# A fused attention kernel: work moved between VectorE and GpSimd at its two ends, and one transpose moved inside its loop

## The chip, the core and the metric

The kernel runs on one core of a Trainium2 chip. The core has five engines that run side by side, each with its own instruction queue: TensorE (PE in the profile) multiplies matrices from SBUF into PSUM; VectorE (DVE) does element-wise work, reductions and 32x32 block transposes; ScalarE (ACT) does exponentials, copies and scalings; GpSimd (POOL) does element-wise work on SBUF; SyncE (SP) mostly issues DMA transfers. ScalarE and GpSimd can issue DMAs from their queues too. Engines wait for each other by semaphores.

The metric is the device time of one execution in microseconds. Times are medians over runs.

## The reference

Self-attention with 16 heads of 32 columns over 8 sequences of 512 rows, with a conditioning vector that is projected by the same W_q and W_k and added to every row of Q and K, and the input added to the result:

```python
Q = _split_heads(x @ Wq.T + bq)
K = _split_heads(x @ Wk.T + bk)
V = _split_heads(x @ Wv.T + bv)
tQ = _split_heads(tokens @ Wq.T + bq)
tK = _split_heads(tokens @ Wk.T + bk)
cQ = Q + tQ
cK = K + tK
scores = jnp.einsum('bhqd,bhkd->bhqk', cQ, cK) / jnp.sqrt(jnp.float32(HEAD_DIM))
attn = jax.nn.softmax(scores, axis=-1)
out = jnp.einsum('bhqk,bhkd->bhqd', attn, V)
...
x = x + out
```

`x` is (8, 512, 512), `tokens` is `cond_1024[:, None, :]` of (8, 1, 512), all float32.

## The kernel before

**Tiles and steps.** The work is cut into 32 tiles `t`: batch `t // 4`, and within it four heads, one from each 128-column block of the model dimension. A tile's K and Q lie transposed in SBUF (`qkT`), so that the four heads sit on the four groups of 32 partitions. Projections are made for pairs of tiles with a scheme of seven half-size products (`product`, L459) whose sums of x blocks (`xc`) and of weight blocks (`wc`) are made by GpSimd (`combine_w`, L353 to L356; `combine_x`, L385 to L389).

**Two ways to the softmax.** For every tile the scores are computed with queries on partitions (`row_scores`, L617), and VectorE takes their negated row maxima (`one_max` L584, `row_max_of` L626). Then the tiles go two ways:
- Odd tiles up to 27 (`BLOCKED`): ScalarE takes the exponentials from these scores (`denominators`, L664) into the `arena`, DMAs regroup them by 32 partitions into `blocks` (`exchange`, L648, on the queues of SyncE and GpSimd), and VectorE transposes the 32x32 blocks in eight units of 128x1024 (`turn_blocks`, L637). TensorE multiplies them by V (`times_v`, L745).
- Even tiles, and the last four: the maxima are split into three bf16 parts (`split_max`, L678 to L681: cast, subtract, cast, subtract, each needing the one before). They are turned by a DMA (`turn_max`, L694), or in the last tiles by TensorE (`transpose_max`, L704, and a copy at L710). The scores are then computed again with keys on partitions, the maxima being added by TensorE (L720, L723), and exponentiated (`exponentials`, L734).

**The loop** runs over steps t = 1 to 28, each with four quarters (items V, q, k, v): quarter 0 multiplies the previous tile's exponentials by V and sends its rows out; quarters 1 to 3 make a product of q, k or v for a later batch. In each quarter the row maxima of one quarter of the next tile are taken, and, where due, a transposition of `blocks`. How many units follow which quarter stands in a small table, `TURNED`, keyed by (step minus tile, quarter). `split_max` for the next tile stands in quarter 2 directly behind its maxima, ahead of that quarter's units.

**Order.** The instruction order on TensorE, ScalarE, VectorE and GpSimd is the program's order, written out by hand; a framework adds the semaphores. Each engine executes its queue strictly in order.

**The start.** The first rows of W_q and the first half of x of batch 0 are loaded by SyncE and ScalarE. GpSimd makes the identity matrix `ident`, then issues DMAs for the two biases (into `cond_sp`, L285) and for the first rows of W_k (`load_first`, L244). VectorE builds `which`, `modulo` and `identb` from memsets and `ident` (L315 to L323), then transposes W_q's rows, the first half of x (L889), W_k's rows (L334), the second half of x (L889), and the conditioning rows (L905), scales the biases (L909, L910), and finishes the conditioning terms `tok` (L860, L861). These are added when q and k are copied out of PSUM (q on VectorE, L415; k on ScalarE, L417). SyncE's queue loads the second half of x, the conditioning vectors (L301), and then the whole of W_q, W_k and W_v.

**The end.** Tiles 30 and 31 have no `blocks`. Their denominators are sums of the four exponential tiles (two halves `pr` each, 128x1024), made by `sum_of` (L1147 for the first two tiles, L1149 for each further one) into `acc` (tile 30) and `acc2` (tile 31), and then multiplied by ones on TensorE (`times_ones`, L755). In `acc`, one half of the first sum is made by GpSimd and the rest by VectorE. GpSimd's last two operations scale tile 30's result and add the residual (L1274, L1275). `send_parts` (L813, L814 on GpSimd) sends tile 29 out just before. Tile 31's result is turned back by TensorE (L1304, L836), divided and stored by VectorE and four DMAs (L1309 to L1321).

Of the kernel before, what the change touches and what calls it, by code (L numbers as in the profile page):

```python
# [9 lines left out]
F32 = mybir.dt.float32  # L10
BF16 = mybir.dt.bfloat16
AF = mybir.ActivationFunctionType
ALU = mybir.AluOpType
# [4 lines left out]
def kernel(  # L18
# [38 lines left out]
    nc = tc.nc  # L57
    P = 128
# [182 lines left out]
    def load_first(n, a, queues):  # L241

        for h in range(HG):
            queues[h].dma_start(  # L244
                first[n][h * BL : (h + 1) * BL].rearrange("p k c e -> p k (c e)"),
                a.rearrange("(k g j) d -> g j k d", g=G, j=BL)[0, :, :, h * P : (h + 1) * P],
            )

    def load_all(to, a, queues, fs=slice(0, NB)):

        for h in range(HG):
            queues[h].dma_start(
                to[h * BL : (h + 1) * BL, fs].rearrange("p f c e -> p f (c e)"),
                spread(a, h * P, NC)[:, fs],
            )
# [23 lines left out]
    load_first("q", Wq, two_queues)  # L279
    load_all(x0, x[0], two_queues, half_of_x[0])  # L280
    nc.scalar.activation(table, table, AF.Exp)
    ident = const.tile([P, P], F32, tag="ident", name="ident")
    make_identity(nc, ident)
    for i, bias in enumerate((bq, bk)):
        nc.gpsimd.dma_start(  # L285
            cond_sp[B + i :: BL, :P], bias.rearrange("(h c) -> h c", h=HG)
        )
    load_first("k", Wk, [nc.gpsimd] * HG)

    def rows_of(n, g):  # L290
        return first[n] if g == 0 and n in first else ws[n].rearrange("p (h g) c e -> p g h c e", g=G)[:, g]
# [7 lines left out]
    for h in range(HG):  # L299
        r = slice(h * P, (h + 1) * P)  # L300
        nc.sync.dma_start(cond_sp[h * BL : h * BL + B, :P], cond[:, r])  # L301
    load_all(ws["q"], Wq, [nc.sync] * HG)
    load_all(ws["k"], Wk, [nc.sync] * HG)
    load_all(ws["v"], Wv, [nc.sync] * HG)
# [6 lines left out]
    nc.vector.memset(m, 0.0)  # L311
    split = [m, m]

    which = const.tile([P, NS], F32, tag="which", name="which")
    nc.vector.memset(which, 0.0)  # L315
    modulo = const.tile([P, BL], F32, tag="modulo", name="modulo")
    for i in range(NS):
        r = slice(i * BL, (i + 1) * BL)
        nc.vector.memset(which[r, i : i + 1], 1.0)
        nc.vector.tensor_copy(modulo[r, :], ident[r, r])  # L320
    condT = early[:, 7, : NC * HD].rearrange("p (c e) -> p c e", e=HD)
    identb = const.tile([P, P], BF16, tag="identb", name="identb")
    nc.vector.tensor_copy(identb, ident)  # L323
    xc = const.tile([P, 4, 2, HS], F32, tag="xc", name="xc")
    vs = [const.tile([P, NS, D], F32, tag=f"v{i}", name=f"v{i}") for i in range(2)]

# [305 lines left out]
    def turn_blocks(t, units):  # L632

        for n in units:
            pr = slice(n % NP * 2, n % NP * 2 + 2)
            e = blocked[t][:, :, n // NP, pr, :].rearrange("p g h s -> p g (h s)")
            nc.vector.transpose(e, e)  # L637
# [207 lines left out]
    def condition(n, gs, pt):  # L845

        i = "qk".index(n)
        r = slice(gs[0], gs[-1] + 1)
        w = len(gs) * HD
        for cc in range(NC):  # L850
            for h in range(HG):
                nc.tensor.matmul(
                    pt[h * HD : (h + 1) * HD, :w],
                    condT[:, cc, :],
                    wT[n][:, cc, :].rearrange("p (g h e) -> p g h e", h=HG, e=HD)[:, r, h, :],
                    start=(cc == 0),
                    stop=(cc == NC - 1),
                )
        t = early[:, 1 + i, :w]
        nc.vector.transpose(t, pt[:, :w])  # L860
        nc.vector.tensor_tensor(  # L861
            tok[:, i, r],
            t.rearrange("p (g b) -> p g b", b=HD)[:, :, :B],
            bias2[:, i, r].unsqueeze(2).broadcast_to([P, len(gs), B]),
            ALU.add,
        )
        if gs[-1] == G - 1:
            nc.gpsimd.tensor_tensor(apart_tok[:, i], tok[:, i, 1::2], tok[:, i, 0::2], ALU.subtract)
# [40 lines left out]
    nc.vector.tensor_scalar(bias2[:, 0, :], condT[:, :, B], 2.0 * SCALE, None, ALU.mult)  # L909
    nc.vector.tensor_scalar(bias2[:, 1, :], condT[:, :, B + 1], 2.0, None, ALU.mult)  # L910
    project(0, "k", pk, two[1])
    condition("q", [0], bank(6))
    condition("k", [0], bank(5))
    project_qk_end(0, "q", pq, two[0])
# [140 lines left out]
            four_products(n, b, r // 2, dens, small, 0)  # L1055
            released(2, 3, 4, 5, 6, 7, 1, 0)

    TURNED = {(-1, 3): 1, (0, 0): 1, (0, 1): 2, (0, 2): 1, (0, 3): 3}
    turned = {1: 1}
    turn_blocks(1, range(1))  # L1060

    def turn_more(t, i):

        for u in (t - 1, t, t + 1):
            if u in BLOCKED and (t - u, i) in TURNED:
                n = turned.get(u, 0)
                turned[u] = n + TURNED[t - u, i]
                turn_blocks(u, range(n, turned[u]))

    ORDERS = {  # L1070
        (1, 0): [],
# [9 lines left out]
    for t in range(1, T - 3):  # L1081
        b, r = divmod(t, G)
        blocks = t in BLOCKED
        w = 0 if blocks else HG
        items = ["V", "q", "k", "v"]
        for i, item in enumerate(items):
            rows = (t + 1, i + 1) if i < 3 else (t + 2, 0)
            begin(w)
            if not blocks:
                exponentials(t, i)  # L1090
            late_first = item in ("v" if blocks else "qkv") and t % 2 == 1
            hold = row_max(*rows, late_first, w)

            def held(i=i, hold=hold):
                hold()
                if i == 2:
                    split_max(t + 1)
                    turn_max(t + 1)

            dens = lambda: denominators(*rows, w)  # L1100
            if item in "qkv":
                products(t, item, blocks, held, dens, nothing)
            else:
                held()
                dens()
                if blocks:
                    weighted(t - 1, banks(4), banks(5), nothing)
                    released(6, 7, 0, 1, 2, 3, 5, 4)
                else:
                    weighted(t - 1, banks(0), banks(1), nothing)  # L1110
                    released(2, 3, 1, 4, 5, 6, 7, 0)
            if i == 0 and r % 2 == 0:
                turn_x(t + NC + 2)
                turn_x(t + NC + 3)
            if i == 0 and r == 1:
                combine_x(b + 1, 1, nc.gpsimd)
            if i == 1 and r == 0:
                combine_x(b + 1, 0, nc.gpsimd)
            if i == 2:
                aparts[t] = masked(t)  # L1120
            turn_more(t, i)
# [33 lines left out]
    def row(i):  # L1155
        turn[0] = 8 + i
# [79 lines left out]
    part_of(t, banks(2), [0])  # L1236
    send_parts(t - 1, den)
    store()
    row(2)
    crossed(t, 2, 3)  # L1240
    split_max(t + 1, nc.vector)
    pa, rest = banks(2), [1, 2, 3]
    times_v(t, 1, pa, rest)

    exponentials(t, 3, (0, 1, 7, 4))
    transpose_max(t + 1, bank(5), nc.vector.tensor_copy)
    times_v(t, 2, pa, rest)
    sum_of(t, acc, 1, nc.vector, [0])
    sum_of(t, acc, 2, nc.vector)

    t = T - 1
    exponentials(t, 0, (2, 3, 0, 1))
    times_v(t - 1, 3, pa, rest)
    nc.vector.tensor_tensor(parts[t - 1], pa, parts[t - 1], ALU.add)
    sum_of(t - 1, acc, 3, nc.vector)
    exponentials(t, 1, (7, 4, 5, 2))
    pv = bank(3)
    times_v(t, 0, pv)
# [1 line left out]
    sum_of(t, acc2, 1, nc.vector)  # L1260
    exponentials(t, 2, (0, 1, 7, 6))
    times_v(t, 1, pv)
    pd = bank(5)
    times_ones(acc, pd, True, True)
    sum_of(t, acc2, 2, nc.vector)
    den = late_part(9).rearrange("p (f e) -> p f e", e=BL)
    nc.vector.transpose(den.rearrange("p f e -> p (f e)"), pd)

# [2 lines left out]
    y30 = late_part(13).rearrange("p (f e) -> p f e", e=BL)  # L1271
    nc.vector.transpose(y30.rearrange("p f e -> p (f e)"), parts[t - 1])
    x30 = xr.pop(t - 1)
    nc.gpsimd.tensor_tensor(y30, y30, rec.broadcast_to([P, NB, BL]), ALU.mult)  # L1274
    nc.gpsimd.tensor_tensor(y30, y30, x30, ALU.add)  # L1275

    def store_30(queue, hs):
        b, g = divmod(t - 1, G)
        for h in hs:
            queue.dma_start(spread(out[b], h * P + g * BL), y30[h * BL : (h + 1) * BL])  # L1280

    store_30(nc.sync, (0, 1))
    exponentials(t, 3, (4, 2, 0, 1))
    times_v(t, 2, pv)
    pd = bank(7)
    times_ones(acc2, pd, True, False)
# [4 lines left out]
    nc.vector.tensor_tensor(part_x, pd, xr[t], ALU.mult)  # L1291
    den = late_part(11)
    nc.scalar.copy(den, pd)
    store_30(nc.scalar, (2,))
    oT = late[0][:, 0, :]
    y = late[0][:, 1, :].rearrange("p (c s) -> p c s", c=NS)
    rec = op.tile([P, NS, HG, 1], F32, tag="rec", name="rec")
# [3 lines left out]
    for i in range(2):  # L1301
        nc.vector.tensor_tensor(oT[:, two[i]], pv[:, two[i]], part_x[:, two[i]], ALU.add)
# [6 lines left out]
    nc.vector.reciprocal(  # L1309
        rec, pi.rearrange("p (c h e) -> p c h e", c=NS, h=HG)[:, :, :, 0:1]  # L1310
    )
# [45 lines left out]
```

## Time and profile before

| | |
|---|---|
| median of 3 runs | 681.87 us (679.42 to 683.93) |
| the profiled execution | 680.71 us |
| its span, first to last instruction | 678.5 us |
| granted TensorE clock, mean | 0.995 |
| busy: TensorE, VectorE, ScalarE, GpSimd | 97%, 85%, 80%, 50% |
| instructions | 22874 |

The profile is one execution, recorded by the hardware. A row of its timeline gives the start and the length in us, the engine, the line of the kernel, the operation with its output and input tiles, the shape and the count (x2 where two of a kind follow each other), and in brackets how long the engine stood idle before and what ended that. An engine name with q is the part that issues DMAs. The chain of waits is followed back from the last instruction: at each step to what released it. A row of the table by stretches gives a window, its length and the busy time of TensorE, its weight loads, VectorE, ScalarE and GpSimd in it, then the granted clock, the share of the DMA engines and GB/s.

### The profile page before, as it was taken

The page shows a single profiled execution, that of the slowest core. Times are in us where ns is not written, and L with a number is a line of the kernel's source. Part 1 is how long each engine was busy: PE and PEld are TensorE (multiplying, and loading weights), DVE is VectorE, ACT ScalarE, POOL GpSimd, SP SyncE. Part 2 cuts the span into 40 slices and gives each one's busy share as a digit, 9 for nine tenths or more (in the row PEclk, how much of TensorE's full clock was granted, in tenths as well). Part 3 has the DMA queues.
Part 4 walks back from the last instruction along what each step waited for, and adds up shares of the span by engine and source line. Part 5 has one row for each costly group of instructions (what it writes and reads, how often), then busy time and mean ns, then how long its engine had stood idle before and what let it go on. Part 6 is the DMA issues. An engine that isn't in the chain of part 4 may idle for free.

```text
span 678.5 us, 22874 instructions
## 1 busy us (share of the span) xinstructions
PE 658.8 (97%) x9100; PEld 312.5 (46%) x9100; DVE 576.4 (85%) x821; ACT 541.9 (80%) x1397; POOL 340.0 (50%) x449
## 2 busy tenths in 40 slices
PE   7989999999999999999999999999999999999993
PEld 6444454544544444454545445444544445444421
DVE  4897988989898888979888897988889797887793
ACT  1568797988979798897979889797988979797771
POOL 5551563565446464465635654464644656352531
PEclk9999999999999999999999999999999999999998
DMA  9719427486483838658383865739386573812002
GB/s 200 133 24 211 127 60 208 95 207 146 123 195 86 221 82 206 147 129 208 74 224 74 209 143 133 196 73 232 73 214 139 132 181 68 222 42 56 16 17 32
DMA packets 140814, 90.85 MB, mean 134 GB/s; under 512 B 117436, under 2 KB 126308, under 8 KB 140708
## 3 DMA queue, kind: packets, MB, share of 16 engines
q1 hardware_dynamic: 132196, 73.78, 46.7%
q0 software_dynamic: 5568, 14.95, 8.6%
q8 instruction: 72, 1.18, 0.8%
q10 hardware_dynamic: 2944, 0.66, 0.4%
q14 instruction: 34, 0.28, 0.1%
HBM read 20.27 MB, written 8.39 MB: 42 GB/s over the span
## 4 chain that ended last, share of the span: by engine, by line
PE 80%; DMA 4%; DVE 3%; SPq 2%; ACT 1%; issue 1%; POOL 0%; DVEq 0%; ACTq 0%
PE psum L459 35%; PE psum L617 17%; PE psum L745 16%; PE psum L723 7%; PE psum L720 3%; DMA blocks<-arena 2%; SPq L648 2%; DMA wT_v<-split 1%; DVE nmax L626 1%; DVE nmax L584 1%; PE psum L1175 1%; PE psum L755 1%; DMA out_dram<-xr 0%; DVE blocks L637 0%; ACT arena L664 0%
## 5 line engine op out<-in xcount | busy, mean ns | idle before, releaser
L664 ACT ACTIVATE psum<-psum,nmax 128x512 f32<-128x512 f32 x256 | 169.1, 664 | 60.0 <-DVE nmax L584 47.5
L584 DVE TENSOR_REDUCE nmax<-psum 128x1 f32<-128x512 f32 x270 | 170.5, 676 | 47.9 <-PE psum L617 47.2
L734 ACT ACTIVATE arena<-psum 128x512 f32<-128x512 f32 x264 | 136.5, 602 | 32.9 <-PE psum L723 25.5
L617 PE MATMUL psum<-kT,qT 32*128 32x512 f32 x1024 | 156.1, 620 | 1.4 <-ACT psum L664 1.4
L664 ACT ACTIVATE arena<-psum,nmax 128x512 f32<-128x512 f32 x224 | 153.0, 704 | 1.2 <-DVE nmax L626 0.3
L626 DVE TENSOR_REDUCE nmax<-psum 128x2 f32<-128x1024 f32 x115 | 139.2, 1211 | 1.1 <-PE psum L617 1.1
L637 DVE STREAM_TRANSPOSE blocks<-blocks 128x1024 f32<-128x1024 f32 x112 | 133.0, 1216 | 0.2
L648 POOL DMA_DIRECT2D blocks<-arena x112 | 55.9, 504 | 76.3 <-ACT arena L664 66.7
L813 POOL TENSOR_TENSOR res<-res,recs 128x512 f32<-128x512 f32 x30 | 31.4, 1048 | 121.7 <-DVE res L812 121.7
L617 PEld LDWEIGHTS psum<-kT,qT 32*128 32x128 f32 x1024 | 58.9, 182 | 64.4 <-issue 28.4
L745 PE MATMUL psum<-arena,v 128*32 128x512 f32 x576 | 69.4, 597 | 0.0
L723 PE MATMUL psum<-qT,kT 32*128 32x512 f32 x528 | 68.1, 587 | 0.0
L745 PE MATMUL psum<-blocks,v 128*32 128x256 f32 x896 | 52.2, 381 | 0.0
L664 ACT ACTIVATION_READ_ACCUMULATOR psum<-psum,nmax 128x1 f32 x256 | 52.1, 204 | 0.0
L459 PE MATMUL psum<-wc_v,xc 128*32 128x256 f32 x768 | 50.6, 381 | 1.4 <-ACT v L497 1.4
L664 ACT ACTIVATION_READ_ACCUMULATOR arena<-psum,nmax 128x1 f32 x224 | 49.7, 222 | 0.0
L459 PE MATMUL psum<-xc,wc_q 128*32 128x256 f32 x720 | 47.4, 381 | 0.0
L459 PE MATMUL psum<-xc,wc_k 128*32 128x256 f32 x720 | 47.4, 381 | 0.0
L814 POOL TENSOR_TENSOR xr<-res,xr 128x512 f32<-128x512 f32 x30 | 38.4, 1281 | 2.4
L812 DVE STREAM_TRANSPOSE res<-psum 128x512 f32<-128x512 f32 x28 | 20.1, 717 | 22.8 <-PE psum L745 22.8
L207 POOL TENSOR_TENSOR xr<-xr,wT_q 128x512 f32<-128x512 f32 x30 | 38.3, 1277 | 0.2
L745 PEld LDWEIGHTS psum<-blocks,v 128*32 128x32 f32 x896 | 27.1, 110 | 24.4 <-ACT arena L734 10.6
(184 smaller groups left out, 933.7 us busy)
## 6 DMA issues: line engine op xcount, KB each, us to landing
blocks<-arena SPq DMA_DIRECT2D x336, 128.0 KB, 3.8
blocks<-arena POOLq DMA_DIRECT2D x112, 128.0 KB, 3.8
xr<-in_x_dram SPq DMA_DIRECT2D x60, 128.0 KB, 2.6
x<-in_x_dram SPq DMA_DIRECT2D x56, 128.0 KB, 3.6
out_dram<-xr SPq DMA_DIRECT2D x56, 128.0 KB, 2.3
w_q<-in_L_cond_Wq_dram SPq DMA_DIRECT2D x4, 256.0 KB, 4.2
w_k<-in_L_cond_Wk_dram SPq DMA_DIRECT2D x4, 256.0 KB
w_v<-in_L_cond_Wv_dram SPq DMA_DIRECT2D x4, 256.0 KB, 8.4
```

Source lines behind the costliest of these rows:

```text
L207: nc.gpsimd.tensor_tensor(xr[t], xr[t], bias, ALU.add)
L459: nc.tensor.matmul(pt[r], still[:, r], moving, start=(kc == kcs[0]), stop=(kc == kcs[-1]))
L584: nc.vector.tensor_reduce(nmax[t][:, qc, j : j + 1, 0], pt, AX.X, ALU.max, negate=True)
L617: nc.tensor.matmul(pt, qkT["q", t][r, qc * P : (qc + 1) * P], qkT["k", t][r, :], start=True, stop=True,)
L626: nc.vector.tensor_reduce(nmax[t][:, qc, pr * 2 : pr * 2 + 2, 0], pt, AX.X, ALU.max, negate=True)
L637: nc.vector.transpose(e, e)
L648: queue.dma_start(to.rearrange("p c h s -> p (c h s)"), of)
L664: nc.scalar.activation(to, of, AF.Exp, bias=nmax[t][:, qc, j, :], accum_out=sums[t][:, qc, j, :],)
L723: nc.tensor.matmul(bank[j], qkT["k", t][r, kc * P : (kc + 1) * P], qkT["q", t][r, :], start=False, stop=True,)
L734: nc.scalar.activation(e[:, i, :], bank[pr * 2 + i], AF.Exp)
L745: nc.tensor.matmul(pt[j * HD : (j + 1) * HD, at], vs[b % 2][:, kc, (g * HG + j) * HD : (g * HG + j + 1) * HD], e, start=(kc == chunks[0]), ...
L814: nc.gpsimd.tensor_tensor(xr[t], y, xr[t], ALU.add)
```

## The change

Four edits:
- At the start, W_k's first rows are issued first on GpSimd's queue, ahead of the identity. The two bias DMAs move to SyncE's queue, behind the conditioning vectors and ahead of W_q. `which`, `modulo` and `identb` are built later on VectorE: behind the scaled biases instead of ahead of the first transposition.
- In the loop, one of the eight units of each odd tile is turned two quarters later, in quarter 2 of its own step instead of quarter 0. (The table gets a third key, a place within the quarter; only the old place is used.)
- Near the end, three more half-sums of tile 30 go from VectorE to GpSimd: the other half of the first sum, and one half of each of the next two. They are queued there behind the residual addition of tile 29.
- At the end, the last two GpSimd operations (tile 30's scaling and residual) go to VectorE, the second of them behind tile 31's last additions, with tile 30's first three stores behind it; and TensorE's last `exponentials` stands ahead of `times_ones(acc)`.

```diff
     nc.scalar.activation(table, table, AF.Exp)
+    load_first("k", Wk, [nc.gpsimd] * HG)
     ident = const.tile([P, P], F32, tag="ident", name="ident")
     make_identity(nc, ident)
-    for i, bias in enumerate((bq, bk)):
-        nc.gpsimd.dma_start(
-            cond_sp[B + i :: BL, :P], bias.rearrange("(h c) -> h c", h=HG)
-        )
-    load_first("k", Wk, [nc.gpsimd] * HG)
...
         nc.sync.dma_start(cond_sp[h * BL : h * BL + B, :P], cond[:, r])
+    for i, bias in enumerate((bq, bk)):
+        nc.sync.dma_start(
+            cond_sp[B + i :: BL, :P], bias.rearrange("(h c) -> h c", h=HG)
+        )
     load_all(ws["q"], Wq, [nc.sync] * HG)
...
-    which = const.tile([P, NS], F32, tag="which", name="which")
-    nc.vector.memset(which, 0.0)
-    modulo = const.tile([P, BL], F32, tag="modulo", name="modulo")
-    for i in range(NS):
-        r = slice(i * BL, (i + 1) * BL)
-        nc.vector.memset(which[r, i : i + 1], 1.0)
-        nc.vector.tensor_copy(modulo[r, :], ident[r, r])
...
-    identb = const.tile([P, P], BF16, tag="identb", name="identb")
-    nc.vector.tensor_copy(identb, ident)
...
     project(0, "k", pk, two[1])
+    which = const.tile([P, NS], F32, tag="which", name="which")
+    nc.vector.memset(which, 0.0)
+    modulo = const.tile([P, BL], F32, tag="modulo", name="modulo")
+    for i in range(NS):
+        r = slice(i * BL, (i + 1) * BL)
+        nc.vector.memset(which[r, i : i + 1], 1.0)
+        nc.vector.tensor_copy(modulo[r, :], ident[r, r])
+    identb = const.tile([P, P], BF16, tag="identb", name="identb")
+    nc.vector.tensor_copy(identb, ident)
     condition("q", [0], bank(6))
...
-    TURNED = {(-1, 3): 1, (0, 0): 1, (0, 1): 2, (0, 2): 1, (0, 3): 3}
+    TURNED = {(-1, 3, 1): 1, (0, 1, 1): 2, (0, 2, 1): 2, (0, 3, 1): 3}
...
     send_parts(t - 1, den)
     store()
+    sum_of(t, acc, 1, nc.gpsimd, [0])
     row(2)
     crossed(t, 2, 3)
+    sum_of(t, acc, 2, nc.gpsimd, [1])
     split_max(t + 1, nc.vector)
...
     exponentials(t, 3, (0, 1, 7, 4))
+    sum_of(t, acc, 3, nc.gpsimd, [1])
     transpose_max(t + 1, bank(5), nc.vector.tensor_copy)
     times_v(t, 2, pa, rest)
-    sum_of(t, acc, 1, nc.vector, [0])
-    sum_of(t, acc, 2, nc.vector)
+    sum_of(t, acc, 2, nc.vector, [0])
...
-    sum_of(t - 1, acc, 3, nc.vector)
+    sum_of(t - 1, acc, 3, nc.vector, [0])
...
     times_v(t, 1, pv)
+    sum_of(t, acc2, 2, nc.vector)
+    exponentials(t, 3, (4, 2, 0, 1))
     pd = bank(5)
     times_ones(acc, pd, True, True)
-    sum_of(t, acc2, 2, nc.vector)
...
-    nc.gpsimd.tensor_tensor(y30, y30, rec.broadcast_to([P, NB, BL]), ALU.mult)
-    nc.gpsimd.tensor_tensor(y30, y30, x30, ALU.add)
+    nc.vector.tensor_tensor(y30, y30, rec.broadcast_to([P, NB, BL]), ALU.mult)
...
-    store_30(nc.sync, (0, 1))
-    exponentials(t, 3, (4, 2, 0, 1))
     times_v(t, 2, pv)
...
-    store_30(nc.scalar, (2,))
...
             untranspose(den, pi)
+    nc.vector.tensor_tensor(y30, y30, x30, ALU.add)
+    store_30(nc.sync, (0, 1))
+    store_30(nc.scalar, (2,))
```

More of the change, by code (lines that the diff above doesn't have):

```diff
@@ L1056, in products, with turn_more @@
             released(2, 3, 4, 5, 6, 7, 1, 0)
-    TURNED = {(-1, 3): 1, (0, 0): 1, (0, 1): 2, (0, 2): 1, (0, 3): 3}
-    turned = {1: 1}
-    turn_blocks(1, range(1))
-    def turn_more(t, i):
+    TURNED = {(-1, 3, 1): 1, (0, 1, 1): 2, (0, 2, 1): 2, (0, 3, 1): 3}
+    turned = {}
+    def turn_more(t, i, slot):
         for u in (t - 1, t, t + 1):
-            if u in BLOCKED and (t - u, i) in TURNED:
+            if u in BLOCKED and (t - u, i, slot) in TURNED:
                 n = turned.get(u, 0)
-                turned[u] = n + TURNED[t - u, i]
+                turned[u] = n + TURNED[t - u, i, slot]
                 turn_blocks(u, range(n, turned[u]))
+    for i in range(NS):
+        for slot in range(2):
+            turn_more(0, i, slot)
     ORDERS = {
@@ L1094, in held @@
             def held(i=i, hold=hold):
+                turn_more(t, i, 0)
                 hold()
@@ L1120 @@
                 aparts[t] = masked(t)
-            turn_more(t, i)
+            turn_more(t, i, 1)
             for what in ORDERS[t % 2, i]:
```

## The prediction

> **What bounds the kernel now.** I read the page's busy shares first, then the chain of waits, then what TensorE waited for, and last the timeline of the two ends.
>
> ```profile
> PE 658.8 (97%) x9100; PEld 312.5 (46%) x9100; DVE 576.4 (85%) x821; ACT 541.9 (80%) x1397; POOL 340.0 (50%) x449
> 73.55 2.63 PE psum L745 x24
> 192.34 2.59 PE psum L745 x24
> 231.78 2.59 PE psum L745 x24
> 626.80 1.85 PE psum L745 x16
> 192.00:232.00 40.00, 40.00 (x576) 18.78 (x572) 35.29 (x50) 33.97 (x89) 21.21 (x28) 1.00 0.65 154
> ```
>
> TensorE is busy for 97% of the span. The L745 rows of the chain of waits open each odd step, so the distance of two of them is the price of two steps: 231.78 - 192.34 = 39.44 us. In the 40 us beside them TensorE is busy for all 40.00, at a granted clock of 1.00. Fourteen such pairs at 39.44 are 552.2 us; the loop takes 626.80 - 73.55 = 553.3. So the loop can give back 1.1 us at most, and everything else that this change can move lies in the 73 us before it and the 52 us after it. TensorE's own waits say where:
>
> ```profile
> PE psum L402 <- DVE wT_k L334: 1.9, 1, 1.9
> PE psum L704 <- DVE split L681: 1.2, 1, 1.2
> PE psum L720 <- DMA wT_v<-split: 0.8, 2, 0.4
> ```
>
> The first is at the start (W_k's first rows come late), the second in the last stretch (the split of the last row maxima), the third twice in the loop. The change has a part for each of the first and third, and moves work beside the second.
>
> **A fact that three parts need: VectorE and GpSimd get in each other's way.**
>
> ```profile
> 12.06 1.26 POOL L385 TENSOR_TENSOR xc<-xT 128x512 f32<-128x512 f32 x1 [7.07 <-DVE xT L889]
> 12.21 1.15 DVE L909 TENSOR_SCALAR bias<-early 128x4 f32<-128x4 f32 x1
> 13.27 0.16 DVE L910 TENSOR_SCALAR bias<-early 128x4 f32<-128x4 f32 x1
> 15.86 1.27 POOL L389 TENSOR_TENSOR xc<-xT,xc 128x512 f32<-128x512 f32 x1
> 16.11 1.03 DVE L861 TENSOR_TENSOR tok<-early,bias 128x8 f32<-128x8 f32 x1
> 648.89 1.21 DVE L626 TENSOR_REDUCE nmax<-psum 128x2 f32<-128x1024 f32 x1
> 650.03 1.26 POOL L814 TENSOR_TENSOR xr<-res,xr 128x512 f32<-128x512 f32 x1
> 650.13 1.22 DVE L678 CAST split<-nmax 128x16 bf16<-128x16 f32 x1
> 651.39 0.18 DVE L679 TENSOR_TENSOR rest<-nmax,split 128x16 f32<-128x16 f32 x1
> 651.61 0.20 DVE L680 CAST split<-rest 128x16 bf16<-128x16 f32 x1
> 651.84 0.23 DVE L681 TENSOR_TENSOR split<-rest,split 128x16 bf16<-128x16 f32 x1
> 652.13 0.40 PE L704 MATMUL psum<-identb,split 128*128 128x128 bf16 x4 [1.22 <-DVE split L681]
> ```
>
> L909 and L910 have one shape: beside a GpSimd operation 1.15 us, free of one 0.16. L861, an addition of 128x8, takes 1.03, where L679, one of 128x16, takes 0.18 with GpSimd still. The two casts L678 and L680: 1.22 and 0.20. Each long one ends within 0.06 us of the end of the GpSimd operation that was under way (13.36 against 13.32, 17.14 against 17.13, 651.35 against 651.29). So a VectorE operation on SBUF operands alone stands still until a running GpSimd operation is done. Reductions from PSUM don't (L626 keeps 1.21 us everywhere).
>
> [...]
>
> **The last stretch: three half-sums to GpSimd.** It matters most.
>
> ```profile
> 646.58 2.36 POOL L1147 TENSOR_TENSOR acc<-arena 128x1024 f32<-128x1024 f32 x1
> 652.98 1.22 DVE L1147 TENSOR_TENSOR acc<-arena 128x1024 f32<-128x1024 f32 x1
> 661.64 2.36 DVE L1149 TENSOR_TENSOR acc<-acc,arena 128x1024 f32<-128x1024 f32 x2
> 660.14 0.86 PE psum L755 x8
> 663.18 0.85 PE psum L755 x4
> 664.05 1.48 PE psum L755 x10
> 666.87 0.44 DVE late L1302
> ```
>
> What it is meant to give: VectorE runs sums from 652.98 to 664.00 and TensorE waits for the last one (L755 continues at 664.05). Three half-sums less are 3 x 1.18 = 3.5 us. From 663.18 to L1302 at 666.87 TensorE has 16 L755 and 8 L745 matmuls. Eight L755 take 0.86 us where nothing waits (the row at 660.14), so 24 need 2.6, and 1.1 us of the 3.7 is idle. That is the whole gain: -1.1 us.
>
> What it costs: on GpSimd's queue the three sums S1, S2, S3 stand directly behind L814, with their inputs done, so S1 starts as L814 ends, at 651.3, and S2 and S3 follow at about 653.7 and 656.1 (2.36 each, three are 7.1). Just there VectorE has the four small operations L678 to L681, each of which needs the one before it, and TensorE's queue stands behind the last (L704 had no slack: it waited 1.22). L678 slips in as L814 ends, as now. L679 comes at 651.39, after S1 has begun, and stands until 653.7; L680 then until S2's end, 656.1; L681 until S3's end, 658.5, and ends some 0.2 later. L704 starts at 658.6 instead of 652.13: +6.5. With the idle 1.1 gone (the sums left to VectorE, six at 1.18, are then far ahead of TensorE), +5.4. If a VectorE operation gets in before one GpSimd operation more, 2.3 less: +3.1 (S3 needs S2's result, which leaves a gap of the kind in which L910 slipped in; L681 comes within 0.03 us of it). I take +5.4; the ends are -1.1 and +5.4.
>
> The last two GpSimd operations go to VectorE: 1.05 and 1.27 us become about 0.7 each. The multiplication lies ahead of L1291, while TensorE is still at work; the addition in the 0.64 us in which VectorE waited for TensorE before L1309 (668.26).
>
> ```profile
> 668.26 0.26 DVE L1309 RECIPROCAL rec<-psum 128x16 f32<-128x16 f32 x1 [0.64 <-PE psum L836]
> 667.98 0.85 SPq L1280 DMA_DIRECT2D out_dram<-late  x2
> 669.08 1.60 SPq L1321 DMA_DIRECT2D out_dram<-late  x2
> ```
>
> So L1309 comes at most 0.1 later, and the two stores of tile 30 on SyncE some 0.3, which their gap to the next pair (668.83 to 669.08) nearly takes up: +0.1. The exponentials of step 31 now stand ahead of `times_ones(acc)` on TensorE: same instructions, in the 1.1 already.
>
> **The start.**
>
> ```profile
> 0.73 0.20 POOL masks.py:197 MEMSET ident<- 128x128 f32 x1 [0.29 <-POOLq L1343]
> 2.76 2.23 POOL L244 DMA_DIRECT2D early<-in_L_cond_Wk_dram  x4
> 7.86 2.27 SPq L252 DMA_DIRECT2D w_q<-in_L_cond_Wq_dram  x4
> 10.08 0.71 DVE L334 STREAM_TRANSPOSE wT_k<-early 128x512 f32<-128x512 f32 x1 [2.55 <-DMA early<-in_L_cond_Wk_dram]
> 10.72 1.26 DVE L889 STREAM_TRANSPOSE xT<-early 128x512 f32<-128x512 f32 x2
> 17.24 0.69 ACT L417 ACTIVATE kT<-psum,tok 128x512 f32<-128x512 f32 x1 [12.55 <-DVE tok L861]
> ```
>
> W_k's four DMAs go out 2.0 us earlier (from 0.73, where GpSimd now begins with the identity, instead of 2.76), so `wT_k` no longer waits to 10.08. Next is late the second half of x: the fourth `w_q` issue waits for its last DMA, and these issues end at 10.13, so it has landed by 9.7 (an estimate). E, the end of `xT`'s second half, moves from 11.98 to about 11.0: 1.0 us earlier, if nothing else holds.
>
> But the `which`/`modulo`/`identb` block now stands on VectorE behind `bias2`, where GpSimd runs its four `xc` sums from E + 0.1 to E + 5.1. Seven operations there use SBUF alone (L909, L910, four copies, one cast), and each that finds GpSimd busy stands to its end: L909 and L910 pass at E + 1.2, one copy each at E + 2.55 and E + 3.8, the rest after E + 5.0: two copies with their memsets, the cast, and L860 and L861 twice, seven operations of 0.2 to 0.3, to about E + 6.5. Before, L861 ended at 17.14 = E + 5.2, and ScalarE's kT (17.24) waits for just that. So 11.0 + 6.5 = 17.5: +0.3 instead of a gain. Bounds: the block unhindered is -2, and the two bias rows landing late on SyncE, where they now stand behind x, is +0.7. Behind them `w_q` to `w_v` are issued two places later, about 0.7 us; `w_q` is used only at 17.8.
>
> **The turning** (128x1024, L637) moves from quarter 0 to quarter 2 of each odd step.
>
> ```profile
> 195.64 1.20 DVE L637 STREAM_TRANSPOSE blocks<-blocks 128x1024 f32<-128x1024 f32 x1
> 203.65 1.22 DVE L637 STREAM_TRANSPOSE blocks<-blocks 128x1024 f32<-128x1024 f32 x1
> 205.34 1.29 DVE L584 TENSOR_REDUCE nmax<-psum 128x1 f32<-128x512 f32 x2 [0.48 <-PE psum L617]
> ```
>
> The maxima of the next two quarters come about 1.0 earlier, so do the split and its DMA, and the two waits of 0.4 go: -0.8, within the 1.1. The second turning in quarter 2 ends at about 205.0 (203.65 - 1.0 + 2 x 1.2), and L584 at 205.34 waits for TensorE anyway. A steady pair stays at 39.44. Ends: -1.1 and 0.
>
> **The sum.** +0.3 - 0.8 + 5.4 + 0.1 = +5.0 us. The profiled execution took 680.71 (its span 678.5), which gives 685.7; on the median of 681.87 (679.42 to 683.93) it would be 686.9. I forecast 686.
>
> **Rivals.** (1) One VectorE operation of the split slips through: end +3.1, sum +2.7, about 684. For it: L681's 0.03 us; against it: S1 and S2 follow each other with no such gap. Chance 0.2. (2) The split goes through whole between L814 and S1, and VectorE's own sums meet the GpSimd ones: three at 2.33 and six at 1.18 one after the other from 651.3 end at 665.4 against 664.00 now; 20 matmuls, 2.15 us, follow that: 667.6 against 666.84, +0.8, sum +0.4, about 682. For it: L679 is only 0.04 behind L678; against: S1 is ready earlier. 0.13. (3) The other side: the sums go their way unhindered, end -1.1. That needs GpSimd's operation to be out of VectorE's way, as its L1147 is beside reductions from PSUM at 646.58. Then sum -1.5, about 680, and down to 677 if the start gains its 2 as well; it decides the sign as soon as L704 comes less than 1.5 us later than now, for all the rest together gives -1.5 (0.3 - 0.8 + 0.1 - 1.1). Against it: L678's 1.22. 0.2. (4) The change does little at both ends (an edge already covered by landing times): about 682, 0.05. The forecast has 0.42.
>
> **Range and chances.** The forecast's own range is 684 to 688 with the start's bounds. Down to rival 3's upper part and with 0.3% of run spread: 679.5 to 689. Less than 1% (6.8 us) is about what a measurement of this kernel can tell from no change; over 688.7 lies only the forecast with a bad start and runs at the upper edge, 0.09; under 675.1 rival 3 with every bound, 0.03; within, 0.88.
>
> **What would show it.** In the profile after: long L679, L680, L681 (their lines shifted), each ending with a GpSimd sum, and TensorE idle some 7 us before the transposes of the split: right; 0.2 us each: rival 3 or 2. The four copies of `modulo` at over 1 us and kT at about 17.5: right; kT at 16 or earlier: the start gained. No L720 wait in the loop and pairs of 39.44: right. The forecast is wrong if the transposes of the split start less than 3 us after the last row maximum ends.

## The result and the profile after

| | before | after |
|---|---|---|
| median (8 runs each, taken beside each other) | 683.44 us | 687.45 us (684.46 to 688.91) |
| ratio, 95% interval | | 1.0058 [1.0037, 1.0079] |
| the profiled execution, its span | 680.71, 678.5 us | 688.91, 686.9 us |
| granted TensorE clock, mean | 0.995 | 0.990 |

The change costs 0.58%, or 4.0 us, with an interval from 2.5 to 5.4. The interval is narrow enough to tell a change well under the 1% that the prediction allowed a measurement, and 687.45 is inside the forecast range. The profiled execution after is the slowest of its eight runs, so its 8.4 us of longer span overstates the change.

Line numbers of the split, TensorE and the products are 9 lower after than before; those of the half-sums are 4 and those of the last additions 3 higher. Four views of the profile after answer to those of before. First the busy shares on the page:

```profile
PE 662.2 (96%) x9100; PEld 313.3 (46%) x9100; DVE 585.7 (85%) x820; ACT 544.4 (79%) x1397; POOL 344.3 (50%) x448
```

Then the waits of TensorE that bear on the change (us in total, times, longest):

```profile
PE psum L695 <- DVE split L672: 7.5, 1, 7.5
PE psum L393 <- DVE xT L880: 2.2, 1, 2.2
PE psum L711 <- DMA wT_v<-split: 1.8, 1, 1.8
```

The wait of 1.2 us for the split has become one of 7.5. TensorE's 3.4 us of additional busy time is just as telling, for it still has 9100 matmuls: some of them became slower. The timeline around the 7.5 us:

```profile
655.12 1.26 POOL L805 TENSOR_TENSOR xr<-res,xr 128x512 f32<-128x512 f32 x1
655.21 1.22 DVE L669 CAST split<-nmax 128x16 bf16<-128x16 f32 x1
656.33 2.35 POOL L1151 TENSOR_TENSOR acc<-arena 128x1024 f32<-128x1024 f32 x1
656.47 2.25 DVE L670 TENSOR_TENSOR rest<-nmax,split 128x16 f32<-128x16 f32 x1
658.63 4.77 POOL L1153 TENSOR_TENSOR acc<-acc,arena 128x1024 f32<-128x1024 f32 x2
658.76 2.28 DVE L671 CAST split<-rest 128x16 bf16<-128x16 f32 x1
661.07 2.41 DVE L672 TENSOR_TENSOR split<-rest,split 128x16 bf16<-128x16 f32 x1
663.54 0.61 PE L695 MATMUL psum<-identb,split 128*128 128x128 bf16 x4 [7.54 <-DVE split L672]
664.08 1.94 PE L736 MATMUL psum<-arena,v 128*32 128x512 f32 x8
```

Each of VectorE's four operations on 128x16 lasts about as long as the GpSimd operation beside it: 1.22 beside L805, then 2.25, 2.28 and 2.41 beside the three half-sums (L1151, and the two of L1153, which end at 663.40). And the eight L736 matmuls behind the wait take 1.94 us. The windows (length, busy time with instruction counts of TensorE, its weight loads, VectorE, ScalarE and GpSimd, then the granted clock, DMA share and GB/s) say what goes with that:

```profile
645.00:655.00 10.00, 10.00 (x106) 4.10 (x102) 7.79 (x11) 7.47 (x16) 9.92 (x9) 1.00 0.17 29
656.00:659.00 3.00, 0.00 (x0) 0.00 (x0) 2.93 (x3) 2.06 (x4) 3.00 (x3) 1.00 0.43 72
659.00:663.50 4.50, 0.00 (x0) 0.00 (x0) 4.45 (x2) 0.00 (x0) 4.32 (x2) 0.50 0.06 10
663.50:669.20 5.70, 5.66 (x32) 1.41 (x32) 1.56 (x2) 0.86 (x2) 0.00 (x0) 0.50 0.00 0
669.20:680.00 10.80, 10.79 (x100) 2.91 (x92) 9.28 (x11) 7.40 (x15) 0.00 (x0) 1.00 0.01 2
```

The granted clock was 1.00 until TensorE had stood idle for 3 us. It was 0.50 for the rest of the wait, and for 5.7 us more after the work had come back.

The chain of waits cuts the span into stretches. The marks of after are these; those of before stand in the prediction.

```profile
74.61 2.59 PE psum L736 x24
...
631.88 1.85 PE psum L736 x16
...
663.54 0.61 PE psum L695 x4
...
670.07 0.86 PE psum L714 x8
...
680.08 0.44 DVE late L1305
```

| stretch | before | after | difference | forecast |
|---|---|---|---|---|
| start to the loop's first mark | 73.55 | 74.61 | +1.1 | +0.3 |
| the loop, to its last mark | 553.25 | 557.27 | +4.0 | -0.8 |
| to the split's transposes (L704, now L695) | 25.33 | 31.66 | +6.3 | +6.5 |
| to the last additions (L1302, now L1305) | 14.74 | 16.54 | +1.8 | -1.1 |
| to the end of the span | 11.6 | 6.8 | -4.8 | +0.1 |
| sum | 678.5 | 686.9 | +8.4 | +5.0 |

The row of the split agrees with the forecast. The last two rows came out quite unlike it. The experiments ask what makes them, and whether the loop's +4.0 belongs to the change.

### The profile page after: what moved, and what is told of

It reads as the page before. It is cut to its first block, busy times and chain, and to the rows that moved or that the text cites. A ratio compares the mean times of both kernels' runs of the same rounds, so it can differ in the third digit from the quotient of the medians.

```text
span 686.9 us, 22873 instructions
## 1 busy us (share of the span) xinstructions
PE 662.2 (96%) x9100; PEld 313.3 (46%) x9100; DVE 585.7 (85%) x820; ACT 544.4 (79%) x1397; POOL 344.3 (50%) x448
## 4 chain that ended last, share of the span: by engine, by line
PE 84%; DMA 5%; DVE 5%; SPq 2%; issue 1%; ACT 1%; DVEq 0%; POOL 0%; ACTq 0%
PE psum L450 37%; PE psum L608 18%; PE psum L736 17%; PE psum L714 7%; DMA blocks<-arena 3%; PE psum L711 3%; SPq L639 2%; PE psum L393 1%; DVE nmax L617 1%; DMA early<-in_x_dram 1%; ACT arena L725 1%; DMA wT_v<-split 1%; DVE blocks L628 1%; DVE nmax L575 1%; PE psum L1179 0%
## 5 line engine op out<-in xcount | busy, mean ns | idle before, releaser
L736 PE MATMUL psum<-arena,v 128*32 128x512 f32 x576 | 69.9, 607 | 0.0
L714 PE MATMUL psum<-qT,kT 32*128 32x512 f32 x528 | 69.6, 596 | 0.0
L736 PE MATMUL psum<-blocks,v 128*32 128x256 f32 x896 | 52.2, 381 | 0.0
L655 ACT ACTIVATION_READ_ACCUMULATOR arena<-psum,nmax 128x1 f32 x224 | 47.7, 213 | 0.0
L803 DVE STREAM_TRANSPOSE res<-psum 128x512 f32<-128x512 f32 x28 | 20.1, 717 | 23.4 <-PE psum L736 23.4
L805 POOL TENSOR_TENSOR xr<-res,xr 128x512 f32<-128x512 f32 x30 | 38.4, 1281 | 2.4
L736 PEld LDWEIGHTS psum<-blocks,v 128*32 128x32 f32 x896 | 26.7, 110 | 24.7 <-ACT arena L725 10.6
```

The source lines that it names most:

```text
L655: nc.scalar.activation(to, of, AF.Exp, bias=nmax[t][:, qc, j, :], accum_out=sums[t][:, qc, j, :],)
L714: nc.tensor.matmul(bank[j], qkT["k", t][r, kc * P : (kc + 1) * P], qkT["q", t][r, :], start=False, stop=True,)
L736: nc.tensor.matmul(pt[j * HD : (j + 1) * HD, at], vs[b % 2][:, kc, (g * HG + j) * HD : (g * HG + j + 1) * HD], e, start=(kc == chunks[0]), ...
L805: nc.gpsimd.tensor_tensor(xr[t], y, xr[t], ALU.add)
```

## The experiments

Each ratio is against runs of the kernel before on the same chip beside it; their medians were 682.60, 682.88 and 683.54 us in the three series. My theory from this profile: the three sums cost the 7.5 us wait and a lowered clock behind it; the end gained 4.8 us because GpSimd no longer works there; start and turning do almost nothing. Against it stood that the wait alone could be the sums' cost, that the 4.8 us at the end could belong to another edit, and that the loop's +4.0 could be the turning's.

**The sums back on VectorE, all else as after.**

```diff
-    sum_of(t, acc, 1, nc.gpsimd, [0])
...
-    sum_of(t, acc, 2, nc.gpsimd, [1])
...
-    sum_of(t, acc, 3, nc.gpsimd, [1])
...
-    sum_of(t, acc, 2, nc.vector, [0])
+    sum_of(t, acc, 1, nc.vector, [0])
+    sum_of(t, acc, 2, nc.vector)
...
-    sum_of(t - 1, acc, 3, nc.vector, [0])
+    sum_of(t - 1, acc, 3, nc.vector)
```

> The changed kernel, with the three half-sums of tile 30 back on VectorE; the rest of the change stays. Theory A: these sums cost some 8 us in the changed kernel (the four operations of the split stand behind them, 6.3; TensorE's lower clock after the idle time, 2.6; less 0.8 of VectorE's time), and the rest of the change gains some 4 (GpSimd's last operation is earlier, and its closing drain no longer ends the execution). So 679.5 us, 4 below the kernel before, and a split of 0.2 us per operation but for its first. Rival B: the loop's later turning is what costs (TensorE lost 4 us in the loop in the one profile of the changed kernel): then it stays at 685 or more. Rival C: both ends are as before without the sums: 683.5.

Measured: 679.09 us, 0.9946 [0.9920, 0.9973]. The four operations of the split take 1.22, 0.18, 0.20 and 0.23 us again. The rest of the change is a gain, and it does not come from the sums.

**The sums alone**, the same lines put into the kernel before.

```diff
+    sum_of(t, acc, 1, nc.gpsimd, [0])
...
+    sum_of(t, acc, 2, nc.gpsimd, [1])
...
+    sum_of(t, acc, 3, nc.gpsimd, [1])
...
-    sum_of(t, acc, 1, nc.vector, [0])
-    sum_of(t, acc, 2, nc.vector)
+    sum_of(t, acc, 2, nc.vector, [0])
...
-    sum_of(t - 1, acc, 3, nc.vector)
+    sum_of(t - 1, acc, 3, nc.vector, [0])
```

> The kernel before, with the three half-sums of tile 30 on GpSimd and nothing else. Theory A: the split's second to fourth operation take 2.3 us each, TensorE idles 7 us before the split's transposes, its granted clock falls, and the time is 8 to 9 us above before: 691 to 692. Rival: without the lower clock +5.4, 689; if one VectorE operation slips between two GpSimd sums, 2.3 less.

Measured: 690.97 us, 1.0121 [1.0092, 1.0149], that is +8.3 us (1.21% of 682.60). Its windows:

```profile
650.00:660.00 10.00, 2.48 (x26) 0.66 (x23) 9.72 (x6) 3.49 (x7) 9.62 (x6) 0.76 0.16 27
660.00:666.00 6.00, 6.00 (x32) 1.32 (x33) 1.56 (x2) 1.28 (x3) 0.00 (x0) 0.54 0.00 0
```

Same wait (TensorE waited 7.5 us for the split), same drop of the clock: the 0.76 and 0.54 are means of these windows, over a clock of 0.50 from 655.3 to 665.5 and 1.00 around it. The +8.3 (6.3 to 10.2 by the interval) agrees with the +6.3 and +1.8 of the table, 8.1.

**The end alone**: the last two GpSimd operations to VectorE, tile 30's first three stores behind them, and the exponentials ahead of `times_ones(acc)`, in the kernel before.

```diff
+    sum_of(t, acc2, 2, nc.vector)
+    exponentials(t, 3, (4, 2, 0, 1))
...
-    sum_of(t, acc2, 2, nc.vector)
...
-    nc.gpsimd.tensor_tensor(y30, y30, rec.broadcast_to([P, NB, BL]), ALU.mult)
-    nc.gpsimd.tensor_tensor(y30, y30, x30, ALU.add)
+    nc.vector.tensor_tensor(y30, y30, rec.broadcast_to([P, NB, BL]), ALU.mult)
...
-    store_30(nc.sync, (0, 1))
-    exponentials(t, 3, (4, 2, 0, 1))
...
-    store_30(nc.scalar, (2,))
...
+    nc.vector.tensor_tensor(y30, y30, x30, ALU.add)
+    store_30(nc.sync, (0, 1))
+    store_30(nc.scalar, (2,))
```

> The kernel before, with only the end changed: tile 30's scaling and residual on VectorE, its stores behind them, the last exponentials ahead of the multiplication by ones. Theory A: GpSimd's closing drain (11.0 us behind its last operation in the profile before) then ends long before the last stores, so the execution ends about 1 us after the last store has landed: 4.8 us less, 678.6. Rival: the 5 us between the last landing and the end belong to the end of any program and stay: 683.5.

Measured: 677.83 us, 0.9929 [0.9903, 0.9954]: -4.8 us, all of the last row of the table. Where that time lay is seen in the windows of the kernel before, at its very end (same columns):

```profile
670.00:672.00 2.00, 0.00 (x0) 0.00 (x0) 0.00 (x0) 0.00 (x0) 0.00 (x0) 1.00 1.02 159
672.00:674.00 2.00, 0.00 (x0) 0.00 (x0) 0.00 (x0) 0.00 (x0) 0.00 (x0) 0.56 0.04 5
674.00:676.00 2.00, 0.00 (x0) 0.00 (x0) 0.00 (x0) 0.00 (x0) 0.00 (x0) 0.50 0.00 0
676.00:678.50 2.50, 0.00 (x0) 0.00 (x0) 0.00 (x0) 0.00 (x0) 0.00 (x0) 0.50 0.00 0
```

The last stores are through by 673, and then for 5 us no engine computes and nothing moves. After the change the stores still move data in the last window:

```profile
685.00:687.00 2.00, 0.00 (x0) 0.00 (x0) 0.00 (x0) 0.00 (x0) 0.00 (x0) 0.50 0.18 28
```

The views leave out what engines do without computing; the trace's records have it. Each engine has a DRAIN instruction at the end of the program, with a barrier of semaphores behind it. GpSimd's DRAIN ends long after its last operation:

| kernel | GpSimd's last operation ends | its DRAIN ends | later by | SyncE's DRAIN, after the last store | span |
|---|---|---|---|---|---|
| before | 667.95 | 677.68 | 9.7 | 672.9 | 678.5 |
| after | 663.40 | 672.96 | 9.6 | 686.1 | 686.9 |
| the end alone | 654.33 | 664.06 | 9.7 | 676.1 | 676.9 |

In all three the span ends 0.8 us behind the later of the two DRAINs. Before, that was GpSimd's, 4.8 us behind SyncE's. (The DRAIN starts while the last operation still runs: before, it lasts 11.0 us, of which 9.7 lie behind that operation. The 11.0 in the expectation above is its whole length. What it waits for the records don't show.)

**One small GpSimd operation at the very end**, added to the kernel after: a copy of 128x32, 0.2 us long, that nobody reads. It puts the suspected cost back without the old work.

```diff
     nc.vector.tensor_tensor(y30, y30, x30, ALU.add)
+    nc.gpsimd.tensor_copy(late_part(12)[:, :BL], y30[:, 0, :])
```

> The changed kernel with one more small copy of 128x32 on GpSimd, behind the residual addition at the very end; its result is used by nothing. Theory A: GpSimd's closing drain starts behind it, at 681.4 by the profile of the changed kernel, takes some 10 us and ends the execution at about 691.5 instead of 686.9: 4 to 5 us more, 692. Rival: the drain's length comes from the 128x512 work before it or from the amount of work in all, and a small copy costs nothing: 687.5.

Measured: 692.39 us, 1.0134 [1.0102, 1.0165], 0.76% or 5.2 us over the ratio of the kernel after. Its timeline shows all that was added:

```profile
681.23 0.21 POOL L1313 COPY late<-late 128x32 f32<-128x32 f32 x1 [18.37 <-DVE late L1312]
```

SyncE's DRAIN ended at 685.9, GpSimd's at 691.0, 9.6 us after the copy, and the span at 691.8. So 0.2 us of GpSimd work cost 5 us. That it is the time of the last GpSimd operation, and not how much GpSimd does, is shown.

**TensorE kept busy through the wait**: 120 small matmuls on a constant, ahead of the split's transposes in the kernel after. Their results are overwritten.

```diff
+    for _ in range(120):
+        nc.tensor.matmul(bank(5)[:, :P], onesb, onesb, start=True, stop=True)
     transpose_max(t + 1, bank(5), nc.vector.tensor_copy)
```

> The changed kernel with 120 small matmuls of ones into the bank that the split's transposes then overwrite, put in front of these transposes, so that TensorE isn't idle while it waits for the split. Theory A: the split is as late as in the changed kernel, but the granted clock stays at 1.00, the matmuls behind the transposes take 1.0 us per eight instead of 1.9, and the time is 2 to 2.6 below the changed kernel: 685. Rival: the longer matmuls come from something else (their inputs, the banks) and stay: 687.5, or longer if the 120 end after the split.

Measured: 683.96 us, 1.0018 [0.9999, 1.0037]: 0.40% or 2.7 us below the kernel after, though it does more. (By the two intervals that difference is uncertain by some 2 us.) Windows and timeline:

```profile
655.00:660.00 5.00, 4.43 (x80) 4.25 (x77) 4.93 (x3) 0.00 (x0) 4.92 (x3) 1.00 0.17 29
660.00:667.00 7.00, 6.79 (x64) 2.00 (x64) 4.36 (x6) 4.00 (x8) 0.07 (x1) 1.00 0.00 0
```

```profile
657.74 2.42 DVE L672 TENSOR_TENSOR split<-rest,split 128x16 bf16<-128x16 f32 x1
660.21 0.40 PE L695 MATMUL psum<-identb,split 128*128 128x128 bf16 x4 [0.78 <-DVE split L672]
660.54 1.07 PE L736 MATMUL psum<-arena,v 128*32 128x512 f32 x8
```

The split is as late as in the kernel after (L672 still takes 2.42 us, and the transposes start 31.7 us behind the loop's last mark in both), but the clock stays at 1.00, and the eight L736 matmuls take 1.07 us again instead of 1.94. The lowered clock is what those 2.7 us were.

**The split on GpSimd, ahead of the three sums**, in the kernel after. This takes the split out of VectorE's queue and leaves the sums where they are.

```diff
-    sum_of(t, acc, 1, nc.gpsimd, [0])
     row(2)
     crossed(t, 2, 3)
+    split_max(t + 1)
+    sum_of(t, acc, 1, nc.gpsimd, [0])
     sum_of(t, acc, 2, nc.gpsimd, [1])
-    split_max(t + 1, nc.vector)
```

> The changed kernel, with the four operations of the last split on GpSimd, ahead of the three half-sums there, instead of on VectorE. Theory A: the four take 0.3 us each, no operation stands behind a half-sum, TensorE waits 1 to 2 us for the split instead of 7.5, its clock stays up, and the time is some 6 to 8 below the changed kernel: 680 to 681; but VectorE's own sums now meet GpSimd's, so not below the kernel with all these sums on VectorE (679.1). Rival: the sums are too slow on GpSimd in themselves (2.35 against 1.18 us) and TensorE waits for the last of them: 684 or more.

Measured: 682.32 us, 0.9981 [0.9960, 1.0002], 5.3 us better than after (0.77%). Its timeline:

```profile
655.86 0.27 POOL L672 TENSOR_TENSOR split<-rest,split 128x16 bf16<-128x16 f32 x1
656.18 0.40 PE L695 MATMUL psum<-identb,split 128*128 128x128 bf16 x4 [1.61 <-POOL split L672]
658.37 5.66 POOL L1153 TENSOR_TENSOR acc<-acc,arena 128x1024 f32<-128x1024 f32 x2
658.44 3.37 DVE L1153 TENSOR_TENSOR acc<-acc,arena 128x1024 f32<-128x1024 f32 x1 [1.34 <-POOL acc L1151]
662.34 2.78 DVE L1153 TENSOR_TENSOR acc<-acc,arena 128x1024 f32<-128x1024 f32 x1
667.31 1.21 DVE L1153 TENSOR_TENSOR acc<-acc,arena 128x1024 f32<-128x1024 f32 x1
```

The split is through at once, and TensorE waits 1.6 us. Now the sums of the two engines meet: VectorE's take 3.37 and 2.78 us instead of 1.21. So even with the split out of the way, the sums on GpSimd show no gain: the ratio is above that of the kernel with the sums on VectorE (0.9946), in intervals that overlap.

**The start alone**: the start's lines of the change, in the kernel before.

```diff
+    load_first("k", Wk, [nc.gpsimd] * HG)
     ident = const.tile([P, P], F32, tag="ident", name="ident")
...
-    load_first("k", Wk, [nc.gpsimd] * HG)
...
+    for i in range(NS):
+        r = slice(i * BL, (i + 1) * BL)
+        nc.vector.memset(which[r, i : i + 1], 1.0)
+        nc.vector.tensor_copy(modulo[r, :], ident[r, r])
```

> The kernel before, with only the start changed: W_k's first rows first on GpSimd's queue, the biases on SyncE's, the block of which, modulo and identb behind the scaled biases. Theory A: the four copies of modulo stand behind GpSimd's sums of x, the first scores start 0.5 us later (18.6 instead of 18.1), and the time is 0.5 to 1 above before: 684.2. Rival: the earlier W_k gains 1 to 2 us: 682.

Measured: 683.69 us, 1.0021 [1.0001, 1.0041]: a small loss, +1.4 us by the ratio, with an interval that nearly touches none.

```profile
15.18 1.14 DVE L909 COPY modulo<-ident 32x32 f32<-32x32 f32 x1
16.43 0.18 DVE L909 COPY modulo<-ident 32x32 f32<-32x32 f32 x1
17.59 0.69 ACT L408 ACTIVATE kT<-psum,tok 128x512 f32<-128x512 f32 x1 [12.90 <-DVE tok L852]
```

A copy takes 1.14 us while GpSimd makes `xc`, and 0.18 when it is done. kT starts at 17.59 instead of 17.24; how far such a difference can be trusted is told below.

**The turning alone**, in the kernel before.

```diff
-    TURNED = {(-1, 3): 1, (0, 0): 1, (0, 1): 2, (0, 2): 1, (0, 3): 3}
+    TURNED = {(-1, 3): 1, (0, 1): 2, (0, 2): 2, (0, 3): 3}
```

> The kernel before, with only the later turning in the loop. Theory A: a steady pair of steps is at TensorE's pace either way (39.44), the two waits for the split's DMA go in most executions: 0 to 1 us less, 682.5. Rival: the later turning makes the loop lose time to late DMAs, as the one profile of the changed kernel lost 4 us in it: 685 or more.

Measured: 682.60 us, 0.9999 [0.9978, 1.0021]. Nothing is seen; the interval is 3 us wide and would hold the forecast gain of 0.8 too. It does exclude the +4.0 of the loop. Twelve runs of this one kernel lie between 680.74 and 686.78, which is the size of scatter that one profiled execution carries; in the 29 runs of the kernel before beside them, the longer times go with a lower granted clock (correlation -0.85). Other profiles with the loop as it is after say the same, here that of the kernel with the small matmuls:

```profile
74.39 2.59 PE psum L736 x24
628.51 1.85 PE psum L736 x16
```

That is 554.1 us. With the old loop, the profile of the sums alone has 73.32 to 628.28, 555.0. So the 557.27 is that one execution's: its three longest pairs take 40.75, 40.66 and 40.93, where an undisturbed pair still takes 39.43.

**Two versions of the rest.** One is the kernel after with the sums on VectorE and `which`, `modulo` and `identb` built ahead of x's transposition, where GpSimd is idle:

```diff
+    which = const.tile([P, NS], F32, tag="which", name="which")
+    nc.vector.memset(which, 0.0)
...
+    nc.vector.tensor_copy(identb, ident)
```

> The changed kernel with the three half-sums back on VectorE, and with the block of which, modulo and identb right behind the transposition of W_q's first rows, where VectorE waits for x anyway. Theory A: the copies meet no sum of GpSimd there, kT starts about 1 us earlier than with the block behind the biases (16.5 to 16.8 instead of 17.5), and the time is 1 us below the same kernel with the late block (679.1): 678. Rival: the two additions of tok then stand behind the sums of x just so, and the time stays at 679.

Measured: 679.48 us, 0.9931 [0.9907, 0.9956].

```profile
6.33 0.18 DVE L896 COPY modulo<-ident 32x32 f32<-32x32 f32 x1
9.69 1.30 DVE L880 STREAM_TRANSPOSE xT<-early 128x512 f32<-128x512 f32 x2 [0.51 <-DMA early<-in_L_cond_bk_dram]
16.33 0.69 ACT L408 ACTIVATE kT<-psum,tok 128x512 f32<-128x512 f32 x1 [11.63 <-DVE tok L852]
```

The copies are at 0.18 us and kT comes at 16.33, 1.5 earlier than after, 0.9 earlier than before, and earlier than in any other profile here (17.24 to 18.63). In the total this is within the scatter.

The other is the kernel before with the end and the turning, and its own start (of the end, only the two residual lines are shown):

```diff
-    TURNED = {(-1, 3): 1, (0, 0): 1, (0, 1): 2, (0, 2): 1, (0, 3): 3}
+    TURNED = {(-1, 3): 1, (0, 1): 2, (0, 2): 2, (0, 3): 3}
...
-    nc.gpsimd.tensor_tensor(y30, y30, x30, ALU.add)
...
+    nc.vector.tensor_tensor(y30, y30, x30, ALU.add)
```

> The kernel before, with the end and the later turning, the start as before and no sum on GpSimd. Theory A: the end gives its 4.8, the turning nothing that can be measured: 677.8, as with the end alone. Rival: the turning gains its 0.8 on top: 677.

Measured: 678.17 us, 0.9933 [0.9908, 0.9958]. It, the end alone (0.9929) and the version above (0.9931) can't be told apart. All three beat both kernels, and the end's edit is what they share.

## Why the prediction was right, and where it was not

**What bounds the kernel, and that all hangs on the two ends: right.** The loop did not move by more than scatter.

**Three operations of the split behind one half-sum each: right, in place and size.** L704's start was put 6.5 us later; it came 6.3 later. The point that rival 1 hung on went as close as was said: L672 came at 661.07, and the third sum had begun at 661.06. It stood for the whole of it. Rival 2's mechanism (the sums of the two engines collide) exists, but only the kernel with the split on GpSimd shows it. Rival 3 is refuted by the rows of 2.25 to 2.41 us.

What was too wide is the conclusion that every VectorE operation on SBUF alone stands still. In the profile after, the first half-sum on GpSimd (L1151) began at 651.66 and took 2.37 us. Beside it a reciprocal of 128x16 (L1003, at 651.97) took 0.24 us and a transposition of 128x512 (L803, at 652.12) 0.66, as long as late in the program with GpSimd idle (0.25 and 0.65). Those that stood were an addition (L861 before, 1.03 us), subtractions (L670 and L672, 2.25 and 2.41), casts (L669 and L671, 1.22 and 2.28), copies (L909, 1.14 to 1.23) and a scaling (L900, 1.16). The split has only such operations, so the forecast did not suffer.

**"L704 starts at 658.6 instead of 652.13: +6.5. With the idle 1.1 gone, +5.4": the step that failed.** It priced the wait at its own length, with TensorE going on behind it as before. From the transposes to the second L723 (L714 after) the same instructions took 3.90 us before (652.13 to 656.03) and 6.53 after (663.54 to 670.07), most of them at a granted clock of 0.50: +2.6. With TensorE kept busy through the wait they took 3.90 again (660.21 to 664.11). The chain of waits has the second L723 before, and L714 in the kernel with the small matmuls:

```profile
656.03 0.86 PE psum L723 x8
...
664.11 0.86 PE psum L714 x8
```

In the profile after, the clock fell 3.0 us into the wait of 7.5 and came back 5.7 us behind it; the 2.6 that this added are about half of the 5.7. The idle time that went was 0.8 (from the second L723 or L714 to the last additions it is 10.8 us before and 10.0 after), not 1.1. Together the last stretch cost 8.1 us in this trace and 8.3 in the kernel with the sums alone, instead of 5.4.

**The tail, "+0.1": the sign was wrong and the size far off, -4.8.** The step costed the two operations as work on the chain of additions and stores, and there it was right: from L1302 (now L1305) to SyncE's DRAIN it is 6.0 us in both kernels. It took for granted that the program ends with its last store. The profile of before had 4.8 us behind that in which nothing ran.

**The start, "+0.3": the mechanism right, the size not settled.** W_k's rows came early (`wT_k` at 9.04 instead of 10.08) and the copies of `modulo` stood still as foreseen, in the timeline after:

```profile
9.04 0.67 DVE L325 STREAM_TRANSPOSE wT_k<-early 128x512 f32<-128x512 f32 x1
...
10.02 1.30 DVE L880 STREAM_TRANSPOSE xT<-early 128x512 f32<-128x512 f32 x2 [0.31 <-DMA early<-in_x_dram]
...
12.84 1.23 DVE L909 COPY modulo<-ident 32x32 f32<-32x32 f32 x1
14.17 1.14 DVE L909 COPY modulo<-ident 32x32 f32<-32x32 f32 x1
15.42 1.14 DVE L909 COPY modulo<-ident 32x32 f32<-32x32 f32 x1
16.66 0.18 DVE L909 COPY modulo<-ident 32x32 f32<-32x32 f32 x1
17.83 0.69 ACT L408 ACTIVATE kT<-psum,tok 128x512 f32<-128x512 f32 x1 [13.13 <-DVE tok L852]
```

kT came at 17.83 where 17.5 was forecast: E, the end of the second half of `xT`, was 10.02 + 1.30 = 11.32 instead of 11.0, and three copies stood instead of two. The +1.1 of the stretch, however, can't be put down to the change from one profile each. In the five profiles with the old start kT begins at 17.24 to 18.17 and the first L745 row at 72.2 to 77.0; in the six with the new start kT begins at 17.52 to 18.63 and the first L736 row at 72.8 to 75.5. A lower clock goes with the later rows: in their first 80 us the five with the old start have none, none, one, two and three stretches at a granted clock of 0.50, and their first L745 row comes at 72.2, 72.4, 74.2, 75.5 and 77.0. So only the runs of the start alone speak, +1.4 us with an interval from 0.1 to 2.8.

**The loop, "-0.8": the waits went, the gain is not seen.** In the profiles of all four kernels with the old table TensorE waits for the split's DMA in the loop, 0.3 to 0.8 us in all. In seven of the eight with the new table it never does; in the profile after it does once, for 1.8, so there the sign that the prediction named (no such wait) did not come. Between the marks of the table above, the loop takes 553.2 to 555.0 us with the old table and 553.2 to 555.3 in those seven. A gain of 0.8 is too small to be seen in that, or to be excluded by the runs.

**Why the total agreed.** In this pair of profiles, from +5.0: the clock adds 2.6, the smaller idle time 0.3 and the start 0.8; the loop's missing gain adds 0.8; the split's 6.3 takes off 0.2 and GpSimd's DRAIN 4.9. That makes +4.4, against a measured 4.0. By the runs, the four edits alone add up to +0.70% (1.21, -0.71, 0.21 and -0.01), against 0.58% [0.37, 0.79]. Two terms of some 3 and 5 us that were not in the sum had opposite signs. The forecast's mechanism was shown; its number was partly luck.

## What to carry to other kernels

When long operations go to GpSimd, list the short operations that depend on each other on VectorE beside them: here three of 0.2 us took 2.25 to 2.41 us each, beside half-sums of 2.34 to 2.35, and cost 6.3. A wait of 7.5 us on TensorE cost 2.6 more than its length here, by the slower clock behind it, and filling it with matmuls that nobody needs gave 2.7 us back. Look at the last rows of a profile, where every engine is idle: in the kernel before, the end was set by GpSimd's DRAIN, 9.7 us behind a residual addition of 1.27 and 4.8 behind SyncE's DRAIN after the last store.

## What was not expected of the hardware

- GpSimd's closing DRAIN ended 9.6 to 9.7 us after its last operation in the records of all twelve kernels, whether that was a 128x1024 addition of 2.3 us or a 128x32 copy of 0.2. It set the end of the span in the five kernels where it ended behind SyncE's DRAIN. Why it takes so long stays open.
- The granted clock stood at 0.50 for 10.2 us in each of the three profiles with a wait of 7.5 us, the last 5.6 to 6.2 of them behind the wait, and the transposes and matmuls slowed with it: four L695 took 0.61 us against 0.40 in the kernel with the small matmuls, eight L736 1.94 against 1.07.
- With both engines adding 128x1024 tiles in SBUF, they ran nearly in turn: in the kernel with the split on GpSimd, two sums of each lie between 658.37 and 665.12, 6.75 us, where two at 2.36 and two at 1.21 one after the other would take 7.1.
